# Fetching the mask's rows of the transposed keys through GpSimd's DMA queue instead of SyncE's

## The chip, the cores and the metric

The kernel runs on one core of one Trainium2 chip. The metric is the device time of one execution in microseconds (us). The profile shows one execution by the hardware profiler; its times are counted from the start of the span.

## The reference

The kernel computes one transformer layer in float32, for 16 batches of 100 tokens of width 256, with a context of 361 rows for each batch: cross attention with 16 heads of width 16, and then a soft mixture of 16 experts with 64 slots each.

```python
x = x + xattn(layernorm(x), ctx, ctx, mask, ...)    # 16 heads, 361 keys
x = x + ffn(layernorm(x), ...)                      # 16 experts, soft slots
...
score = einsum('bhqd,bhkd->bhqk', q, k) / sqrt(HD)
score = score + (1.0 - mask) * -1000000000.0
alpha = softmax(score, axis=-1)
```

The mask has one value for each batch and key. It is added to the scores of every head and every query.

## The kernel before

**Stages and order.** The 16 batches are taken in five groups of 2, 2, 4, 4 and 4. For every batch the kernel projects queries and keys and then runs four "units" (`cb` = 0 to 3, four heads each): the scores' maxima (matmuls L681, reduction L686 on VectorE), the corrected queries (L694, L696), the exponentials (L704, L712) and the product with the values (L726). An output projection follows (`out_work`, L627), a second layernorm, and the dispatch to the experts' slots (`dispatch_quarter`: L821, softmax with L881, transposes L889, L899). The experts of a group (L1150 gate and up projections, L1110 down projection) run while the attention of the next group is worked on. All of it is put in order when the program is built: a planner keeps an estimated clock for each engine (`Clock`), holds every piece of work as a generator that tells when it is ready (`Task`), and always takes the next ready one. So each engine has a fixed list of instructions and goes through it in that order; it waits at an instruction until what that one needs is there. Before the first expert the planner fills TensorE's waiting time with matmuls that nobody reads (`warm_up`, L1201), and these too are fixed in number.

**How the mask gets into the scores.** The keys are kept transposed in `kT`, 128 partitions by two halves `oc`, two parities `par` and 361 keys. Each group of 32 partitions holds two heads, of which a parity keeps one and blanks the other, so that blank rows can carry other things: row `MAXROW` carries the maxima, row `MASKROW` the mask. `late_loads` turns the mask into (mask - 1) * 1e9 and stores it in device memory (`mrow_d`, L292). For every batch, `key_work` computes the keys on TensorE (`k_ps`, L546), writes `kT` for `oc` = 0 by VectorE (L557) and for `oc` = 1 by ScalarE (L562), and then issues four small DMAs at L573, one for each (`par`, `oc`), each of which copies the batch's 361 mask values to the four rows that blank heads leave free (5.6 KB). They are issued in the order (0,0), (0,1), (1,0), (1,1), each after the engine that wrote that part of `kT`. The unit `cb` = 2 * `oc` + `par` reads the part that belongs to it.

**Queues.** Before the change SyncE (SP) issues these four DMAs, and nearly all others: the context `c_sb` (L180, L181), the tokens `acc` (L171), the experts' weights `w_all` in pieces of 512 KB (L1084), their biases (L1090) and the results (L1055). GpSimd (POOL) issues only nine small or middling DMAs at the start (mask, biases, layer norm parameters, one scale; L213 to L232) and the slot embeddings `se` (L340, 1 MB, in `parameter_work`), which VectorE's statistics read first (L370, called in `slot_work` at L396). `se` lies in the buffer `ring`, and the profile names it so. GpSimd also computes: reciprocal square roots (L381, helper `rstd`), the scaling of the attention's result (L618), the bias L513, the dispatch weights (L881) and the combine weights (L978, L1004 to L1008).

```python
def parameter_work():
    yield 14.0, 0
    nc.gpsimd.dma_start(
        se, slot_embeds.rearrange("e s d -> (e s) d").rearrange("(c p) d -> p c d", p=P)
    )
```

**Buffers.** `kT` and `c_sb` have two buffers each; for the second group (batches 2 and 3) the keys lie in a part of `ring` instead. Six slots hold experts' weights, and a weight's load is issued as soon as the slot's last reader is done.

Of the kernel before, what the change touches and what calls it, by code (L numbers as in the profile page):

```python
# [118 lines left out]
def xattn_ffn_kernel(  # L119
# [27 lines left out]
    nc = tc.nc  # L147
# [9 lines left out]
    def mm_tile(name):  # L157
        return ps_mm.tile([P, 512], F32, tag="mm", name=name)
# [19 lines left out]
    def load_kv(b):  # L178
        c_sb = two.tile([P, 3, D], F32, tag="c_sb", name="c_sb")
        nc.sync.dma_start(c_sb[:KC, 0:2, :], kv[b, : 2 * KC].rearrange("(c p) d -> p c d", p=KC))  # L180
        nc.sync.dma_start(c_sb[: S2 - 2 * KC, 2, :], kv[b, 2 * KC :])  # L181
        loads[b] = c_sb
        kv_t[b] = max(ck.t["PE"] + 6.0, 5.5)
# [332 lines left out]
    def key_work(b):  # L516

        yield 5.5, 0
        if b + 1 < B and b + 1 not in loads:
            load_kv(b + 1)  # L520
        c_sb = loads[b]
        cT = const.tile([P, KD, S2], F32, tag="cT", name="cT")
        t = [0.0, 0.0]
        for kd in range(KD):
            yield kv_t[b], 1
            ps = mm_tile("c_t")
            for c in range(3):
                n = KC if c < 2 else S2 - 2 * KC
                nc.tensor.transpose(  # L529
                    ps[:, c * KC : c * KC + n],  # L530
                    c_sb[:n, c, kd * P : (kd + 1) * P],
                    ident[:n, :n],
                )
            nc.scalar.copy(cT[:, kd, :], ps[:, :S2])
            t = ck.copy(361, ck.run("PE", 0.33, ck.bank(), kv_t[b]))
            ck.free(t)
        early = group_of[b] == 1
        kT = early_kT[b % 2] if early else None
        for oc in range(KD):
            yield (lambda: max(t, par_t[0], 7.0) if kT is not None or keys_fit(b) else NEVER), 1  # L540
            if kT is None:
                live.add(b)
                kT = two.tile([P, KD, 2, S2], F32, tag="kT", name="kT")
            ps = mm_tile("k_ps")
            for kd in range(KD):
                nc.tensor.matmul(  # L546
                    ps[:, :S2],
                    lhsT=w_sb["wk"][:, kd, oc * P : (oc + 1) * P],
                    rhs=cT[:, kd, :],
                    start=kd == 0,  # L550
                    stop=kd == KD - 1,
                )
            tk = ck.pe(722, t, ck.bank())
            for par in range(2):
                one = slice(par, par + 1)
                if oc == 0:
                    nc.vector.tensor_scalar(  # L557
                        kT[:, oc, par, :], ps[:, :S2], sel[:, one], kb[:, oc, one], ALU.mult, ALU.add
                    )
                    tk = ck.psum_dve(361, tk)  # L560
                else:
                    nc.scalar.activation(  # L562
                        kT[:, oc, par, :],
                        ps[:, :S2],
                        AF.Identity,
                        bias=kb[:, oc, one],
                        scale=sel[:, one],
                    )
                    tk = ck.copy(361, tk)
            ck.free(tk)  # L570
        for par in range(2):
            for oc in range(KD):
                nc.sync.dma_start(  # L573
                    kT.rearrange("(r c) k t s -> r c k t s", c=32)[:, MASKROW[par], oc, par, :],
                    mrow_d[b : b + 1].to_broadcast([4, S2]),
                )
        keys[b] = (kT, tk + 3.0)
        vp = values_of[b] = (early_vpads if early else vpads)[b % 2]
        for c in range(3):

            yield t, 1
            ps = mm_tile("v_ps")
            for kd in range(KD):
                nc.tensor.matmul(  # L584
                    ps[: KC + 1, :D],
                    lhsT=cT[:, kd, c * KC : c * KC + KC + 1],
                    rhs=w_sb["wv"][:, kd, :],
                    start=kd == 0,
                    stop=kd == KD - 1,
                )  # L590
            nc.vector.tensor_tensor(
                vp[: KC + 1, c, :, 0:4:3, :],
                ps[: KC + 1, :D].rearrange("p (x k w) -> p x k w", k=2, w=HD),
                bcs["bv"][: KC + 1, :].rearrange("p (x k w) -> p x k w", k=2, w=HD),
                ALU.add,
            )
            tv = ck.psum_dve(256, ck.pe(512, t, ck.bank()))
            ck.free(tv)
        values_t[b] = tv
# [146 lines left out]
    def keys_fit(b):  # L746
        return len(live) < 2
# [6 lines left out]
    def units(g):  # L754
        last = None

        def finish(u):
            u.values()
            if u.cb == 3 and u.b + 1 in group and u.b + 2 in group:
                fill.append(Task(key_work(u.b + 2), ck))  # L760

        group = range(starts[g], starts[g] + GROUPS[g])
        for b in group:
            for cb in range(4):
                yield (lambda: max(keys[b][1], qps[b][1]) if b in keys and b in qps else NEVER), 0
                yield free_t[0], 0
                u = Unit(b, cb)
                u.maxima()
                if cb == 0 and b % 2 == 1 and b + 1 in group:
                    fill.append(Task(query_work(b + 1), ck))  # L770
                if last:
                    lt = last
                    yield (lambda: values_ready(lt)), 1
                    finish(last)
                yield u.t, 0
                u.queries()
                yield u.t, 0
                u.exponentials()
                last = u
        yield (lambda: values_ready(last)), 1  # L780
        finish(last)
# [422 lines left out]
    group = 0  # L1204
    fill.append(Task(query_work(0), ck))
    fill.append(Task(key_work(0), ck))
    fill.append(Task(bias_work(), ck))
    fill[0].step()
    late_loads()
    while streams["experts"]:  # L1210
# [3 lines left out]
        if group < len(GROUPS) and not streams["units"]:  # L1214
            if group in accs:
                b0 = starts[group]
                if group > 1:
                    fill.append(Task(query_work(b0), ck))
                    fill.append(Task(key_work(b0), ck))
                    fill.append(Task(key_work(b0 + 1), ck))  # L1220
                elif group == 0:
                    fill.append(Task(key_work(1), ck))
                    fill.append(Task(parameter_work(), ck))
                    fill.append(Task(early_work(), ck))
                    fill.append(Task(slot_work(), ck))
                    load_x(1)
                    fill.append(Task(query_work(2), ck))
                    fill.append(Task(key_work(2), ck))
                    fill.append(Task(key_work(3), ck))
                xns[group] = const.tile([N, NG, D], F32, tag="xn", name="xn")  # L1230
                xnTs[group] = const.tile([P, KD, NG * N], F32, tag="xnT", name="xnT")
                streams["units"] = Task(units(group), ck)
                group += 1
# [102 lines left out]
```

## Time and profile before

| | |
|---|---|
| time, median of 3 runs | 1220.04 us (1219.3 to 1221.12) |
| time of the profiled execution | 1216.74 us |
| its span | 1214.9 us |
| TensorE busy | 1191.2 us (98%) |
| VectorE, ScalarE, GpSimd busy | 559.2, 552.1, 148.5 us (46%, 45%, 12%) |
| mean DMA rate | 119 GB/s |
| DMAs `kT<-mrow_d`, and `ring<-mrow_d` for batches 2 and 3 | 56 and 8, by SP |

The profiled execution has 1.84 us outside its span and lies 3.30 us below the median of the runs. TensorE (PE, with PEld for its weight loads) is busy nearly throughout. The other engines have a lot of idle time, which counts only where TensorE, in its fixed order, comes to an instruction whose input is late. In a line of the timeline the first number is the start, the second the duration; in square brackets stand the idle time just before it and what is taken to have ended it. The rows of the DMA issues end with the KB of one and, for GpSimd's queue, the median time from issue to landing.

### The profile page before, as it was taken

Reading aid. Unit: us, or ns where it says so; the run is one execution under the profiler, and the core shown is the slowest. Engines: PE = TensorE matmul, PEld = TensorE weight load, DVE = VectorE, ACT = ScalarE, POOL = GpSimd, SP = SyncE. Lnnn points to the kernel's source line nnn. Section 1 sums busy time; section 2 is a strip of 40 time slices with the busy share of each in tenths; the row PEclk is TensorE's granted clock in tenths of the full one; section 3 lists DMA queues with packets and bytes.
Section 4 is the critical chain, followed back from the end, with each engine's and each line's share of the span. In section 5 each row is a group of like instructions: output and inputs, shape, how many; then the busy total and the mean of one; then the engine's idle time right before and its main releaser. Section 6 shows DMA issues by size and latency. Waiting matters only on the chain.

```text
span 1214.9 us, 24560 instructions
## 1 busy us (share of the span) xinstructions
PE 1191.2 (98%) x10107; PEld 931.7 (77%) x10107; DVE 559.2 (46%) x1328; ACT 552.1 (45%) x1140; POOL 148.5 (12%) x229
## 2 busy tenths in 40 slices
PE   7998999999999999999999999999999999999998
PEld 5877877877787777777777677887778778877876
DVE  5664555557545556744554423447222233322222
ACT  2436454466454466654544446674111347511110
POOL 2110210014000013231000000034000013200000
PEclk9999999999999999999999999999999999999999
DMA  6103556442566441133223142324354332344441
GB/s 161 39 28 94 168 193 196 156 135 73 163 220 192 139 145 44 41 104 113 81 95 110 36 148 71 109 87 130 122 168 141 125 109 83 121 136 147 147 141 53
DMA packets 104184, 144.71 MB, mean 119 GB/s; under 512 B 6284, under 2 KB 62792, under 8 KB 104072
## 3 DMA queue, kind: packets, MB, share of 16 engines
q1 hardware_dynamic: 103216, 141.60, 37.2%
q8 instruction: 80, 1.31, 0.5%
q0 software_dynamic: 576, 1.27, 0.4%
q10 hardware_dynamic: 280, 0.26, 0.1%
q14 instruction: 32, 0.26, 0.1%
HBM read 141.45 MB, written 1.66 MB: 118 GB/s over the span
## 4 chain that ended last, share of the span: by engine, by line
PE 94%; DVE 2%; ACT 2%; DMA 1%; issue 0%; POOL 0%; ACTq 0%; POOLq 0%; DVEq 0%
PE dn L1110 19%; PE gp L1150 19%; PE up L1150 18%; PE sl L899 5%; PE po L1032 4%; PE at L704 4%; PE at L681 4%; PE lg L821 3%; PE k_ps L546 3%; PE cx L726 3%; PE v_ps L584 3%; PE warm L1201 2%; PE o_ps L627 1%; PE d_t L889 1%; DMA kT<-mrow_d 1%; PE c_t L529 1%
## 5 line engine op out<-in xcount | busy, mean ns | idle before, releaser
L1166 DVE SCALAR_TENSOR_TENSOR hT<-up,parT,ge 128x256 f32<-128x256 f32 (+1 forms) x320 | 119.9, 425 | 282.3 <-PE up L1150 194.5
L1150 PE MATMUL gp<-ring,w_all 128*128 128x256 f32 (+1 forms) x1280 | 248.5, 341 | 0.2 <-ACT xnT L657 0.2
L1150 PE MATMUL up<-ring,w_all 128*128 128x256 f32 (+1 forms) x1280 | 246.6, 340 | 0.1
L1161 ACT ACTIVATE ge<-gp,parT 128x256 f32<-128x256 f32 (+1 forms) x320 | 116.7, 429 | 261.5 <-PE gp L1150 260.9
L1110 PE MATMUL dn<-w_all,hT 128*64 128x256 f32 x2048 | 231.8, 381 | 0.0
L1150 PEld LDWEIGHTS gp<-ring,w_all 128*128 128x128 f32 x1280 | 202.7, 191 | 27.5 <-issue 6.4
L1150 PEld LDWEIGHTS up<-ring,w_all 128*128 128x128 f32 x1280 | 203.9, 191 | 21.6 <-issue 1.1
L1110 PEld LDWEIGHTS dn<-w_all,hT 128*64 128x64 f32 x2048 | 142.7, 137 | 76.8 <-issue 7.0
L686 DVE TENSOR_REDUCE mxp<-at 100x4 f32<-100x1444 f32 x64 | 106.3, 1661 | 37.5 <-PE at L681 36.6
L1119 DVE TENSOR_TENSOR ring<-dn,bd_bc 128x512 f32<-128x512 f32 x64 | 44.1, 689 | 153.8 <-PE dn L1110 153.8
L1161 ACT ACT_TABLE_LOAD x61 | 78.3, 1283 | 41.6 <-PE gp L1150 34.8
L712 ACT ACTIVATE aT<-at 121x1200 f32<-121x1200 f32 x64 | 74.9, 1170 | 44.5 <-PE at L704 40.7
L618 POOL TENSOR_TENSOR cxs<-cxs,rs 128x100 f32<-128x100 f32 x63 | 25.1, 399 | 412.1 <-DVE rs L615 336.7
L712 ACT ACT_TABLE_LOAD x39 | 50.0, 1283 | 31.4 <-PE at L704 20.0
L899 PE MATMUL sl<-disp,xn 100*128 100x256 f32 x256 | 61.4, 385 | 1.1 <-ACT disp L892 1.1
L881 POOL TENSOR_TENSOR d_ex<-d_ex,d_sm 128x400 f32<-128x400 f32 x28 | 23.7, 852 | 306.6 <-DVE d_sm L878 259.3
L1032 PE MATMUL po<-ring,lg_all 128*100 128x256 f32 x256 | 59.3, 381 | 0.0
L735 ACT COPY cxs<-cx 128x100 f32<-128x100 f32 x64 | 15.5, 242 | 87.8 <-PE cx L726 87.7
L899 PEld LDWEIGHTS sl<-disp,xn 100*128 100x128 f32 x256 | 47.1, 190 | 9.7 <-ACT disp L892 1.8
L704 PEld LDWEIGHTS at<-q,kT 32*121 32x121 f32 x1344 | 41.2, 182 | 16.9 <-issue 7.9
L704 PE MATMUL at<-q,kT 32*121 32x100 f32 x1344 | 50.6, 280 | 0.7 <-DVE q L696 0.6
L1032 PEld LDWEIGHTS po<-ring,lg_all 128*100 128x100 f32 x256 | 41.7, 167 | 12.0 <-DVE hT L1166 0.5
(148 smaller groups left out, 1323.4 us busy)
## 6 DMA issues: line engine op xcount, KB each, us to landing
w_all<-in_L_ffn_Wg_dram SPq DMA_DIRECT2D x80, 512.0 KB
w_all<-in_L_ffn_Wu_dram SPq DMA_DIRECT2D x80, 512.0 KB
w_all<-in_L_ffn_Wd_dram SPq DMA_DIRECT2D x80, 512.0 KB
bd_bc<-in_L_ffn_bd_dram SPq DMA_DIRECT2D x80, 64.0 KB
c_sb<-in_ctx_dram SPq DMA_DIRECT2D x16, 240.0 KB
c_sb<-in_ctx_dram SPq DMA_DIRECT2D x16, 121.0 KB
acc<-in_x_dram SPq DMA_DIRECT2D x8, 200.0 KB
out_dram<-acc SPq DMA_DIRECT2D x8, 200.0 KB
```

The source lines that it names most:

```text
L546: nc.tensor.matmul(ps[:, :S2], lhsT=w_sb["wk"][:, kd, oc * P : (oc + 1) * P], rhs=cT[:, kd, :], start=kd == 0, stop=kd == KD - 1,)
L681: nc.tensor.matmul(self.at[:N, r, :S2], lhsT=self.q[rows], rhs=self.k[rows], start=True, stop=True)
L686: nc.vector.tensor_reduce(mxv[:, :, m : m + 1], self.at[:N, :, :S2], AX.X, ALU.max, negate=True)
L704: nc.tensor.matmul(self.at[: KC + 1, r, c * N : (c + 1) * N], lhsT=self.k[rows, c * KC : c * KC + KC + 1], rhs=self.q2[rows], start=True, ...
L712: nc.scalar.activation(self.aT[: KC + 1], self.at[: KC + 1, :, : 3 * N], AF.Exp)
L899: nc.tensor.matmul(sl[:, kd * 256 : (kd + 1) * 256], lhsT=xns[g][:, b0 + i, kd * P : (kd + 1) * P], rhs=disp[:, i, :], start=True, stop=True,)
L1032: nc.tensor.matmul(pos[i][:N, :D], lhsT=lg_all[:, slot, 2 * c + i, :], rhs=eouts_of(g, q)[:, c, 2 * p + i, :], start=c == 0, stop=c == 1,)
L1110: nc.tensor.matmul(dn[S * x : S * x + S, i * D : (i + 1) * D], lhsT=hts[x][fc // FB][0].rearrange("p (f b s) -> p f b s", f=FB, s=S)[:, fc ...
L1119: nc.vector.tensor_tensor(eouts_of(g, q)[:, j // 2, 2 * half : 2 * half + 2, :], dn.rearrange("p (b d) -> p b d", d=D), biases[k // 2].uns ...
L1150: nc.tensor.matmul(ps[:, f * T : (f + 1) * T], lhsT=w[:, kd, fc * P : (fc + 1) * P], rhs=slots_of(g, q)[:, j, kd].rearrange("p b s -> p (b ...
L1161: nc.scalar.activation(ge[:, cols], ps[:, cols], AF.Gelu, bias=col(8, e, fc))
L1166: nc.vector.scalar_tensor_tensor(out=hT[:, cols], in0=ps[:, cols], scalar=col(NPAR, e, fc), in1=ge[:, cols], op0=ALU.add, op1=ALU.mult,)
```

## The change

For every batch but the first, the four DMAs at L573 are issued by GpSimd instead of SyncE:

```diff
         for par in range(2):
             for oc in range(KD):
-                nc.sync.dma_start(
+                (nc.gpsimd if b else nc.sync).dma_start(
                     kT.rearrange("(r c) k t s -> r c k t s", c=32)[:, MASKROW[par], oc, par, :],
                     mrow_d[b : b + 1].to_broadcast([4, S2]),
                 )
```

These are 15 times four DMAs. The planner does not count DMAs, so the order of the instructions on TensorE, VectorE and ScalarE stays as it was. SyncE's list loses the 60 DMAs. GpSimd's list gets them at the place where `key_work` reaches them; for batch 1 that is ahead of the load of the slot embeddings (L340), for batches 6 and 10 between two of the multiplications L881, and for batch 12 ahead of an L381.

## The prediction

> **What bounds the kernel now.** I read the page first: TensorE (PE) is busy for 98% of the span and makes up 94% of the chain that ended last. So only time in which PE stands still can be won, and only new stillness of PE can be lost.
>
> ```profile
> PE 1191.2 (98%) x10107; PEld 931.7 (77%) x10107; DVE 559.2 (46%) x1328; ACT 552.1 (45%) x1140; POOL 148.5 (12%) x229
> PE 94%; DVE 2%; ACT 2%; DMA 1%; issue 0%; POOL 0%; ACTq 0%; POOLq 0%; DVEq 0%
> ```
>
> Then PE's timeline, for the maxima L681, the first readers of the mask's rows. Of 64 units four waited, and three of these are the first unit of a batch whose rows had just been ordered:
>
> ```profile
> 19.70 0.87 PE L681 MATMUL at<-kT,qp 32*100 32x361 f32 x8 [0.35 <-DMA kT<-mrow_d]
> 212.50 0.87 PE L681 MATMUL at<-kT,qp 32*100 32x361 f32 x8 [0.18 <-DMA kT<-mrow_d]
> 397.22 0.87 PE L681 MATMUL at<-kT,qp 32*100 32x361 f32 x8 [1.00 <-DVE vpad L591]
> ```
>
> These are batches 0, 4 and 8. The third names VectorE's `vpad`, which L681 doesn't read. What it needs of VectorE, `qp` of L502, was done by 396.10, before PE fell idle at 396.22; a DMA is left. I take all three as waits for the rows: 0.35 + 0.18 + 1.00 = **1.53 us**, all that the mask's rows cost PE (batch 12's first unit, at 578.93, waited for nothing). PE's list of waits has no other DMA but that for `para` at the start: no weight was ever late.
>
> SP's timeline, and the chain at batch 4, show why rows of 5.6 KB take so long: they are queued behind 2 MB of weights and context.
>
> ```profile
> 387.39 0.63 SPq L1084 DMA_DIRECT2D w_all<-in_L_ffn_Wd_dram  x1
> 388.08 0.51 SPq L1090 DMA_DIRECT2D bd_bc<-in_L_ffn_bd_dram  x1
> 388.63 0.60 SPq L180 DMA_DIRECT2D c_sb<-in_ctx_dram  x1
> 389.27 0.37 SPq L181 DMA_DIRECT2D c_sb<-in_ctx_dram  x1
> 390.52 3.41 SPq L573 DMA_DIRECT2D kT<-mrow_d  x4
> ```
> ```profile
> 206.62 5.74 DMA kT<-mrow_d
> ```
>
> The chain gives 5.74 us from the first issue to landing at batch 4; batch 8's must have been about 397.1 - 390.5 = 6.6. By the windows the DMA engines were 0.75 to 1.06 busy in every microsecond from 390 to 395.
>
> **Part 1: the rows on GpSimd's queue.** One issue there costs 0.50 to 0.54 us (the four L228), about SP's 0.48 to 0.60. What counts is the time to landing. The trace has this for GpSimd's small DMAs at the start only:
>
> ```profile
> ring<-in_L_ffn_norm_b_dram POOLq DMA_DIRECT2D x1, 1.0 KB, 5.7
> sc_bc<-in_L_ffn_scale_dram POOLq DMA_DIRECT2D x1, 0.5 KB, 3.4
> ```
>
> 3.4 us is the last of them, issued at 8.06 with nothing of its own queue just ahead; 5.7 and up to 6.3 (mask) are those behind one another, with the DMA engines saturated from 4 to 8 us. So the bounds are 3.4 and 6.3. I take 4.5, nearer to 3.4, since the four rows have nothing ahead of them in their own queue.
> - Batch 4: ordered at 206.6, landed at 211.1 (bounds 210.0 and 212.9), PE there at 212.32: **-0.18** (bounds -0.18, +0.4).
> - Batch 8: ordered at 390.5, landed at 395.0 (393.9 to 396.8), PE there at 396.22: **-1.00** (bounds -1.00, -0.4). The next on PE, `c_t` of batch 9, would come at 397.1 and reads context that went out just ahead of the old rows and so landed by 397.1: nothing to 0.1.
> - Batch 12: 572.9 + 4.5 = 577.4, PE at 578.93: 0 (up to +0.2). Batch 2: GpSimd comes free from an L618 at 81.91, rows at 86.4, PE at 88.39: 0. The others have over 9 us to their first L681.
>
> The row first: two small transfers behind SP's burst took 5.74 and 6.6 us. The Trainium skill, "DMA: Bandwidth & Descriptors", section "Queues, rings and completion order", says that each DMA engine alternates between queues packet by packet; by this the rows pass the weights, and the sum is the one above. Its section "Issuing engines are not separate DMA queues" speaks against the change: all queues share 16 engines and another issuer saves only issue time; by this batches 4 and 8 gain nothing. The trace of before cannot decide it.
>
> **Part 2: GpSimd's own work behind the rows.** GpSimd executes in order; the four issues (4 x 0.52 = 2.1 us) also wait for `kT` from VectorE and ScalarE, and what stands next waits with them. 60 issues add 31 us to an engine busy 148.5 of 1214.9. Next in line, by batch:
> - 6 and 10: an L881. For 6 the rows start at 275.26 and end at 277.34; L881 started at 276.21, so it is 1.13 late and ends at 278.2. Its reader, the transposes L889, comes on PE at 280.21: 2.0 left. Batch 10 has the same distances (459.99, 460.94, 464.94). Cost 0.
> - 11: ScalarE's first `kT` part ends at 499.2, the last issue at 500.8; L881 started at 501.01. Cost 0.
> - 12: ScalarE writes `kT` from 574.61 to 575.80; the issues end at 576.8; L381 started at 574.76, so it is 2.05 late and ends at 577.36. Its reader on VectorE, L648, started at 577.77: 0.4 left. Cost 0 (+0.4 at an issue of 0.7).
> - 2, 3, 4, 5, 7, 8, 9, 13, 14, 15: GpSimd's next work started over 2 us after the rows would be issued. Cost 0.
>
> **Part 3: the slot embeddings.** The load L340 was issued at 9.77. Now the rows of batch 1 stand ahead of it and wait for `kT` (VectorE till 24.17, ScalarE from 24.29 to 25.48): issues at 23.65, 24.95, 25.47, 25.99, and L340 at 26.5. Its reader is VectorE:
>
> ```profile
> 9.77 0.94 POOL L340 DMA_DIRECT2D ring<-n_L_ffn_slot_embeds_dram  x1
> 35.51 0.41 DVE L370 BATCH_NORM_STATS2 st<-ring 128x6 f32<-128x256 f32 x1
> 36.94 1.67 DVE L686 TENSOR_REDUCE mxp<-at 100x4 f32<-100x1444 f32 x1 [0.27 <-PE at L681]
> ```
>
> Two things follow. First, from 10 to 20 us the 1 MB no longer shares the engines with SP's first rows (12.71 to 19.57 for batch 0 in the chain; 2.09 MB moved in these 10 us by the windows, half of it `se`). Batch 0's rows then come before PE does: **-0.35** (bound 0). Second, `se` must land by 35.5. It took 10.0 us, which gives 36.5; L686 has 0.27 of slack, so a landing at X costs X - 35.8: +0.7. But SP, no longer held at L573 until 26.6, issues its three weight loads at 17.8 to 19.3; at the 310 GB/s of the windows from 28 to 34 these, `c_sb` and `acc` (2.3 MB) are through by about 27, and `se` has the engines alone: 1.05 MB / 310 = 3.4, plus the 3.4 of a small DMA, lands at 33.3. I take **0**, bound +0.7.
>
> **Part 4: SP without the rows.** It waited 127 us at L573; now the loads behind go out earlier (at 76 instead of 94.5 before the first experts). PE waited for no weight, so nothing is won; later in the mixed phase loads are held by weight slots anyway.
>
> **Sum:** -0.18 - 1.00 - 0.35 = -1.53 us on the profiled 1216.74 (span 1213.4, time 1215.2). PE's later work is PE-bound, so I keep it all. The same off the median of the runs: 1220.04 - 1.53 = **1218.5 us**, -0.13%. All bounds at their worst: +0.4 - 0.4 + 0.2 + 0.4 + 0.7 = +1.3, so 1221.3.
>
> **One more row.** GpSimd's issues stayed at 0.50 to 0.56 us while VectorE was 1.68 of 2.0 us busy with memsets (2 to 4 us). The Trainium skill, "SBUF — State Buffer", section "SBUF: two separate sides", warns that VectorE's two-port operations shut GpSimd out while it writes descriptors: 620 ns become 3100. By that a batch's issue could grow by 10 us and hold L381 and L881; no row here shows it.
>
> **Rivals.**
> - *The rows land no sooner* (5.5 to 6.3 us, the engines being the same). Batch 4 0 to +0.4, batch 8 -1.0 to -0.4, batch 12 up to +0.2, batch 0 -0.35: about 1219.6. For it: the rows at 5.7 to 6.3; against: 3.4. Chance 25%.
> - *The slot embeddings come late* and VectorE stands at L370: the slower side. If the loads are not through and `se` shares with the 1.9 MB of weights and context, it needs 3.4 + 2.98 MB / 310 = 13.0 (X = 39.5, +3.7) up to 10.0 + 6.2 = 16.2 (X = 42.7, +6.9); with the -1.5 that is 1222.2 to 1225.4. It decides from a landing 10.8 us after the issue (X = 37.3). Against: SP is free from 17.8 on. Chance 15%.
> - *GpSimd is held longer*: issues twice as long (4.2 us a batch) make batch 12's L381 2.1 later (+1.7) and `se` too (28.6 + 6.8 = 35.4, or +2.8 at 10.0): 1220.2 to 1223.0. Chance 10%.
> - *More is won*, by waits that I don't see: below 1217.6, 5%.
> - The forecast as it stands: 45%, though the runs' spread (1219.3 to 1221.12) can carry it past a bound.
>
> **Range and chances.** 0.2% is 2.44 us, about what a measurement of this kernel can tell from no change. Faster by more, below 1217.6: 5% and as much again by spread, 10%. Slower by more, above 1222.5: most of the second rival and some of the third, 18%. Within: 72%. The range, 1217.4 to 1223.5, holds the forecast, the first rival, and the lower parts of the second and third.
>
> **What would show it.** After: no idle time before the L681 near 212 and 396 and at 19; L340 near 26.5, L370 not waiting; L881 of batches 6 and 10 about 1.1 later and L889 not. Wrong if L370 or L648 waits, if the rows' issues on GpSimd exceed 0.6 us, or if the L681 still wait.

## The result and the profile after

The change makes the kernel slower: 1224.88 us (median of 15 runs, 1221.84 to 1228.52) against 1220.04 us for the kernel before (15 runs beside them), ratio 1.0045, 95% interval 1.0032 to 1.0058. That is 4.84 us more, where 1.53 us less was predicted, and it lies outside the predicted range. The profiled execution of after took 1222.76 us with a span of 1221.0 us; that of before had 1214.9 us.

The page of after looks almost like the page of before. TensorE has 1.9 us more of busy time, GpSimd 35.3 us more:

```profile
PE 1193.1 (98%) x10107; PEld 933.0 (76%) x10107; DVE 560.3 (46%) x1328; ACT 553.5 (45%) x1140; POOL 183.8 (15%) x289
PE 93%; DVE 2%; DMA 2%; ACT 2%; issue 0%; POOL 0%; ACTq 0%; POOLq 0%; DVEq 0%
```

PE's timeline shows the loss at two first units and one transpose (start, duration, and in brackets the idle time ahead of it with what ended it):

```profile
214.01 0.87 PE L681 MATMUL at<-kT,qp 32*100 32x361 f32 x8 [2.21 <-DMA kT<-mrow_d]
400.15 1.07 PE L681 MATMUL at<-kT,qp 32*100 32x361 f32 x8 [2.00 <-DMA kT<-mrow_d]
583.90 0.36 PE L653 MATMUL xn_t<-ident,xn 100*128 100x100 f32 x2 [0.84 <-DVE xn L648]
```

The waits that the change was to take away at batches 4 and 8 have grown from 0.18 and 1.00 us to 2.21 and 2.00. TensorE's matmuls are the same 10107 in the same order, so comparing equal instructions in the two traces tells where the 6.1 us of the spans lie: at batch 0's L681 after is 0.56 us ahead of before (19.14 against 19.70), at batch 4's L681 it is 1.51 us behind (214.01 against 212.50), at batch 8's 2.93 (400.15 against 397.22), at an L704 soon after it 4.52 (407.82 against 403.30), at batch 12's L653 5.55 (583.90 against 578.35), and 6.1 at the end.

**The rows land late.** The chain of waits holds the stretch from the first row's issue to its landing, at batch 4 and at batch 8. It is this first row, for `cb` = 0, that PE waits for:

```profile
206.37 7.51 DMA kT<-mrow_d
...
392.72 7.30 DMA kT<-mrow_d
```

On SP's queue batch 4's first row took 5.74 us. Yet GpSimd's queue isn't slow as such: over all 52 rows for `kT` the page gives a median of 2.2 us from issue to landing (last number), and the DMA view of 204 to 216 us alone gives 7.0 as the median of batch 4's four rows.

```profile
kT<-mrow_d POOLq DMA_DIRECT2D x52, 5.6 KB, 2.2
```
```profile
kT<-mrow_d POOLq DMA_DIRECT2D x4, 5.6 KB, 7.0
```

**SP runs ahead.** SP's timeline of after at batch 8 shows what fills the DMA engines in these 7 us. Before, the contexts of batch 10 and the next Wg were issued at 395.65, 396.06 and 396.52, behind the rows:

```profile
390.51 0.63 SPq L180 DMA_DIRECT2D c_sb<-in_ctx_dram  x1
391.18 0.38 SPq L181 DMA_DIRECT2D c_sb<-in_ctx_dram  x1
391.66 0.84 SPq L180 DMA_DIRECT2D c_sb<-in_ctx_dram  x1
392.56 0.37 SPq L181 DMA_DIRECT2D c_sb<-in_ctx_dram  x1
394.91 0.39 SPq L1084 DMA_DIRECT2D w_all<-in_L_ffn_Wg_dram  x1
```

The second pair (361 KB) now goes out ahead of the first row, which GpSimd issues at 392.72, and 512 KB of Wg only 2.2 us after it. The windows show the longer burst at batch 4; the columns are the window, its length, the five engines' busy time, then PE's clock, the DMA engines' share and GB/s. Before:

```profile
210.00:211.00 1.00, 1.00 (x7) 0.94 (x6) 0.37 (x1) 0.00 (x0) 0.00 (x0) 1.00 0.87 176
211.00:212.00 1.00, 1.00 (x7) 0.79 (x5) 0.41 (x2) 0.52 (x1) 0.00 (x0) 1.00 0.51 129
212.00:213.00 1.00, 0.82 (x10) 0.29 (x8) 0.93 (x5) 0.52 (x1) 0.00 (x0) 1.00 0.10 33
```

After:

```profile
210.00:211.00 1.00, 1.00 (x7) 0.84 (x6) 0.49 (x1) 0.36 (x1) 0.00 (x0) 1.00 1.05 246
211.00:212.00 1.00, 0.80 (x4) 0.36 (x2) 0.81 (x2) 0.44 (x2) 0.00 (x0) 1.00 1.08 240
212.00:213.00 1.00, 0.00 (x0) 0.00 (x0) 0.93 (x5) 0.23 (x1) 0.42 (x1) 1.00 1.04 231
213.00:214.00 1.00, 0.00 (x0) 0.02 (x1) 0.08 (x1) 0.00 (x0) 1.00 (x2) 1.00 0.84 207
```

**The clock drops behind the second wait.** In after's windows from 400 us, PE is busy, but at half the clock:

```profile
400.00:401.00 1.00, 0.85 (x8) 0.29 (x8) 0.00 (x0) 0.00 (x0) 0.72 (x1) 0.84 0.62 212
401.00:402.00 1.00, 1.00 (x8) 0.85 (x5) 0.74 (x1) 0.00 (x0) 0.00 (x0) 0.50 0.09 31
402.00:403.00 1.00, 1.00 (x7) 1.00 (x6) 1.00 (x2) 0.81 (x2) 0.00 (x0) 0.50 0.00 0
403.00:404.00 1.00, 1.00 (x7) 1.00 (x6) 0.24 (x1) 0.11 (x1) 0.00 (x0) 0.50 0.00 0
404.00:405.00 1.00, 1.00 (x10) 1.00 (x10) 0.00 (x0) 0.00 (x0) 0.00 (x0) 0.95 0.06 16
```

0.16 + 3 x 0.50 + 0.05 = 1.71 us of full clock are missing. That accounts for the step from 2.93 to 4.52 us (1.59).

**Batch 12.** GpSimd's timeline of after has the rows, then the L381 and L513 that stood behind them. L381's input (L378) was done by 579.15; L381 starts 2.65 us later:

```profile
580.10 1.68 POOL L573 DMA_DIRECT2D kT<-mrow_d  x3 [1.77 <-ACT kT L562]
581.80 0.57 POOL L381 TENSOR_TENSOR rstd<-rstd,neghalf 100x1 f32<-100x1 f32 x1
582.34 1.25 POOL L513 TENSOR_TENSOR acc<-acc,bo_bc 100x512 f32<-100x512 f32 x1
```

So L648 on VectorE, which had run alone before (second line), now runs beside L513 and takes over three times as long (first line, after; in run 2 below it is 1.35 us beside L513 too, in run 8 it is 0.40 behind it):

```profile
582.41 1.35 DVE L648 TENSOR_SCALAR xn<-acc,mv,rstd 100x256 f32<-100x256 f32 x1
```
```profile
577.77 0.40 DVE L648 TENSOR_SCALAR xn<-acc,mv,rstd 100x256 f32<-100x256 f32 x1
```

### The profile page after: what moved, and what is told of

It is laid out like the page before. It is cut to its first block, busy times and chain, and to the rows that moved or that the text cites. A ratio compares the mean times of both kernels' runs of the same rounds, so it can differ in the third digit from the quotient of the medians.

```text
span 1221.0 us, 24571 instructions
## 1 busy us (share of the span) xinstructions
PE 1193.1 (98%) x10107; PEld 933.0 (76%) x10107; DVE 560.3 (46%) x1328; ACT 553.5 (45%) x1140; POOL 183.8 (15%) x289
## 4 chain that ended last, share of the span: by engine, by line
PE 93%; DVE 2%; DMA 2%; ACT 2%; issue 0%; POOL 0%; ACTq 0%; POOLq 0%; DVEq 0%
PE dn L1110 19%; PE gp L1150 19%; PE up L1150 18%; PE sl L899 5%; PE po L1032 4%; PE at L704 4%; PE at L681 4%; PE lg L821 3%; PE k_ps L546 3%; PE cx L726 3%; PE v_ps L584 3%; PE warm L1201 2%; DMA kT<-mrow_d 1%; PE d_t L889 1%; PE o_ps L627 1%; PE c_t L529 1%
## 5 line engine op out<-in xcount | busy, mean ns | idle before, releaser
L881 POOL TENSOR_TENSOR d_ex<-d_ex,d_sm 128x400 f32<-128x400 f32 x28 | 23.8, 855 | 297.8 <-DVE d_sm L878 254.4
L704 PEld LDWEIGHTS at<-q,kT 32*121 32x121 f32 x1344 | 41.1, 182 | 16.9 <-issue 8.2
L681 PE MATMUL at<-kT,qp 32*100 32x361 f32 x448 | 48.7, 504 | 4.6 <-DMA kT<-mrow_d 4.2
L704 PE MATMUL at<-q,kT 32*121 32x100 f32 x1344 | 50.6, 280 | 0.7 <-DVE q L696 0.6
```

Source lines behind the costliest of these rows:

```text
L681: nc.tensor.matmul(self.at[:N, r, :S2], lhsT=self.q[rows], rhs=self.k[rows], start=True, stop=True)
L704: nc.tensor.matmul(self.at[: KC + 1, r, c * N : (c + 1) * N], lhsT=self.k[rows, c * KC : c * KC + KC + 1], rhs=self.q2[rows], start=True, ...
```

## The experiments

Three theories stood at the start. **A**: the rows share the DMA engines with SP's burst, and SP, released from the rows, sends more into that burst, so the rows land later. **B**: GpSimd's queue is late by itself when the DMA engines are full. **C**: the loss is spread over GpSimd's own work behind the rows. Every kernel was timed in five rounds beside the kernel before (in the three sessions its median was 1218.08, 1219.18 and 1218.58 us). All differ from it only in what the diffs show.

**1. One row stays on SP.** The fourth row of each batch holds SP until the last part of `kT` is written.

```diff
-                nc.sync.dma_start(
+                (nc.gpsimd if b and (par, oc) != (1, 1) else nc.sync).dma_start(
```

> Of the four rows of a batch only the last, (par, oc) = (1, 1), stays on SyncE (for every batch); the other three of batches 1 to 15 are on GpSimd. SyncE is again held until the keys are written, so the context of the batch after next and the next weights go out as late as before the change. Theory A (the rows land late because the released SyncE lengthens the burst that they share the DMA engines with): the rows of batches 4 and 8 land when the burst of before ended, so the waits at L681 near 214 and 400 shrink from 2.21 and 2.00 us to 0 to 0.5 and 0.5 to 1.0; no low clock near 400; 1219.5 to 1221.5 us. Theory B (GpSimd's queue is slow under load by itself, whatever SyncE does): both waits stay near 2 us, 1222.5 to 1225 us.

Measured: 1222.66 us, ratio 1.004 (1.0024 to 1.0056). PE waited 2.73 us at batch 4 (chain: 8.03 us from issue to landing) and 1.37 at batch 8. Holding SP in this way didn't help, which at this point spoke for B. But SP's timeline showed that it had not been held long: the contexts of batch 6 went out at 210.77, 2.5 us after the first row (before: 5.3 us after it), and the next Wg at 211.70. The windows show what that meant: in the 8.03 us up to the landing the DMA engines moved 2.08 MB at a share of 1.01, against 1.92 MB in the 7.51 us of after and 1.35 MB at a share of 0.82 in the 5.74 us of before. So what SP issues in the first microseconds behind the row can still delay it. Runs 5 and 9 take this up.

**2 to 4. Which batches, and which queue.** Rows of batches 0, 4, 8 on SP and the others on GpSimd; only 4 and 8 on GpSimd; only 4 and 8 on ScalarE's queue.

```diff
-                nc.sync.dma_start(
+                (nc.gpsimd if b not in (0, 4, 8) else nc.sync).dma_start(
```

> The rows of batches 4 and 8, the first of their groups, are back on SyncE; all others but batch 0 stay on GpSimd. If the loss sits at these two units (theories A and B alike): the waits at L681 are 0.2 and 1.0 us again, the 0.35 of batch 0 stays won, the 0.8 at batch 12 stays lost: 1219.5 to 1221.5 us. Theory C (the loss is spread, by GpSimd's own work that stands behind the rows): 1223 us or more.

```diff
-                nc.sync.dma_start(
+                (nc.gpsimd if b in (4, 8) else nc.sync).dma_start(
```

> The counterpart: only the rows of batches 4 and 8 are on GpSimd, all others on SyncE. Theories A and B: waits of about 2.2 and 2.0 us at L681, a low clock after one or both of them in some executions, 1222 to 1225.5 us; the wait of 0.84 at L653 (batch 12) is gone and the 0.35 of batch 0 is back. Theory C: within 1 us of before.

```diff
-                nc.sync.dma_start(
+                (nc.scalar if b in (4, 8) else nc.sync).dma_start(
```

> Only the rows of batches 4 and 8 are moved, to ScalarE's queue, which is a hardware queue like SyncE's; SyncE is released there as in the change. Theory A: ScalarE's rows share the same lengthened burst, waits of 1 to 2.5 us at L681, 1221.5 to 1225 us. Theory B (a trait of GpSimd's software queue, for instance its completion): the rows land within 5 us, waits under 0.3 us, 1218.5 to 1220 us.

Measured: 1220.80 us, ratio 1.0021 (1.0007 to 1.0034), for all but 0, 4 and 8 on GpSimd; 1222.70 us, 1.004 (1.0025 to 1.0055), for 4 and 8 alone on GpSimd; 1219.46 us, 1.0013 (1.0001 to 1.0024), for 4 and 8 on ScalarE. So two batches of fifteen can carry nearly all of the loss (4.6 of 4.8 us), which is against C (the second run's 2.7 and the third's 4.6 us add up to more than the 4.8 of the change; with their intervals, 0.9 to 4.1 and 3.0 to 6.7 us, they can be parts of it). PE's timeline of the third run has the waits of after:

```profile
215.71 0.87 PE L681 MATMUL at<-kT,qp 32*100 32x361 f32 x8 [2.25 <-DMA kT<-mrow_d]
402.27 0.87 PE L681 MATMUL at<-kT,qp 32*100 32x361 f32 x8 [1.87 <-DMA kT<-mrow_d]
```

With ScalarE as the issuer the waits are 0.34 and 0.30 us. (The time still is 1.4 us above before, 0.1 to 2.9 by the interval; no wait in this trace shows where.) The short waits too fit B, but SP's list explains them otherwise, and shows what the rows do on SP. In the compiled program the DMAs of SP and ScalarE take eight semaphores in turn (the traces' records number them 100 to 107), and each DMA waits until the one eight before it has landed; GpSimd's DMAs have semaphores of their own (108 to 115). Four rows on SP or ScalarE take four of these eight places, so that the next context and the next Wg wait for later transfers to land. Rows on GpSimd take none. In the fourth run the contexts of batch 6 went out at 211.58 and 214.34, in the third at 207.50 and 208.14. So the fourth run keeps the brake, and A and B were still not told apart.

**5. GpSimd's queue with SP's places kept.** SP copies four other rows of `kT` into a spare tile where its own rows stood.

```diff
+    spare = const.tile([4, KD, 2, 340], F32, name="spare")
...
-                nc.sync.dma_start(
+                (nc.gpsimd if b in (4, 8) else nc.sync).dma_start(
...
+                if b in (4, 8):
+                    nc.sync.dma_start(
+                        spare[:, oc, par, :],
+                        kT.rearrange("(r c) k t s -> r c k t s", c=32)[:, 5, oc, par, :340],
+                    )
```

> Rows of batches 4 and 8 on GpSimd's queue as in the third run, and SP copies four rows of kT (340 columns of them, partition 5 of each 32) into a spare tile at the place where its own four rows stood. Nothing of the output changes. So SP again waits for the copies of kT there, and again has four small transfers among the eight that it may have under way (each of its transfers waits until the one eight before it has landed). A (the rows land late because SP, released, sends contexts and weights into the burst sooner): the contexts of batch 6 go out some 5 us after the first row, as before (211.90 after 206.62), the rows land under 6.5 us after their issue, PE's two waits at L681 are under 1.2 us each, and the kernel is within 2 us of before (third run: 4.6 above). B (GpSimd's queue is late by itself when the DMA engines are full): the rows land 7 us or more after their issue, PE waits some 2 us at 214 and at 400, and the kernel stays 3 to 5 us above before.

Measured: 1219.24 us, ratio 1.0001 (0.999 to 1.0013). Four more transfers for each of the two batches, and the loss of the third run no longer shows in the time. SP's timeline, the first row at batch 4 by the chain (the third run's line ahead of this run's) and PE's timeline of this run:

```profile
207.76 3.96 SPq L579 DMA_DIRECT2D spare<-kT  x4
213.38 0.34 SPq L180 DMA_DIRECT2D c_sb<-in_ctx_dram  x1
```
```profile
208.03 7.55 DMA kT<-mrow_d
```
```profile
208.02 6.45 DMA kT<-mrow_d
```
```profile
214.61 0.87 PE L687 MATMUL at<-kT,qp 32*100 32x361 f32 x8 [1.16 <-DMA kT<-mrow_d]
399.70 0.87 PE L687 MATMUL at<-kT,qp 32*100 32x361 f32 x8 [0.57 <-DMA kT<-mrow_d]
```

The rows are on the same queue as in the third run, and the first lands in 6.45 us instead of 7.55 (5.87 instead of 7.17 at batch 8; by the median of the four rows 5.1 instead of 7.2, and 4.7 instead of 6.8), because the contexts come 5.4 us after the first row instead of 0.5 us before it. A holds, and B falls as the cause of the loss. But the first row lands no sooner than on SP, where it took 5.74 us in before and 5.96 in run 8: PE's waits of 1.16 and 0.57 us add up to 1.73, more than the 1.18 of before, so a small part of B may be left.

**6. Contexts out of the burst, rows on SP.** The load of a batch's context moves to the place behind the rows two batches earlier. The planner's due time for the context (`kv_t`) keeps its old place and value, so that the orders on TensorE, VectorE, ScalarE and GpSimd stay the same.

```diff
-        kv_t[b] = max(ck.t["PE"] + 6.0, 5.5)
+        if b < 2:
+            kv_t[b] = max(ck.t["PE"] + 6.0, 5.5)
...
-        if b + 1 < B and b + 1 not in loads:
-            load_kv(b + 1)
+        if b + 1 < B and b:
+            kv_t[b + 1] = max(ck.t["PE"] + 6.0, 5.5)
...
+        if b + 2 < B:
+            load_kv(b + 2)
```

> All rows on SP as before; the context of batch b + 2 is loaded behind batch b's rows instead of batch b + 1's ahead of them, so that the context of batch 5 (361 KB) has landed long before the burst at batch 4. The orders on TensorE, VectorE, ScalarE and GpSimd stay the same. A (what is in the burst ahead of the rows sets when they land): 361 KB less at the 300 GB/s of the burst is 1.2 us, so the rows of 4 and 8 land some 1.2 us sooner; PE's waits there (0.18 and 1.00 before) fall to what VectorE ends next, 0 to 0.7 as in the second run: 0 to 1 us faster than before, no more. B (the queue's own manner): says nothing of rows on SP, no change.

Measured: 1217.28 us, ratio 0.9987 (0.9976 to 0.9998), 1.9 us below before's median: more than expected, but the interval reaches into it. PE's timeline shows no idle time ahead of the two L681 (L684 in this file):

```profile
216.04 0.87 PE L684 MATMUL at<-kT,qp 32*100 32x361 f32 x8
...
400.36 0.87 PE L684 MATMUL at<-kT,qp 32*100 32x361 f32 x8
```

So the waits that the change was after, the 1.18 us at batches 4 and 8, go away when 361 KB are taken out from ahead of the rows, without another queue. Whether the time falls by as much isn't shown (see the end).

**7. The same contexts, rows of 4 and 8 on GpSimd.** The sixth run's diff and the third's together.

> The same move of the contexts, with the rows of batches 4 and 8 on GpSimd's queue (third run with 361 KB less ahead of the rows, but SP as free as there). A: the rows land about 1 us sooner than in the third run (7.0 us there), PE's waits at batches 4 and 8 fall from 2.25 and 1.87 to about 1 each, and the kernel is 1 to 3 us above before. B: landing 7 us and waits of about 2 us as in the third run, 3 to 5 us above before.

Measured: 1221.45 us, ratio 1.0023 (1.0012 to 1.0034), 2.3 us above before, as A said. The waits were a miss for A as I had sized it, though: 1.82 and 2.36 us, with the first rows landing in 7.12 and 7.66 us (medians of the four 6.2 and 6.4). SP was free here, and sent batch 6's context at 206.71 and 207.50 and, in the place of the other context, the next Wg (512 KB) at 208.25, all ahead of the first row at 208.82. Taking one transfer out of the burst doesn't help when nothing keeps the next from taking its place.

**8. The twelve batches that have time.** Rows of 0, 4, 8, 12 on SP, the others on GpSimd.

```diff
-                nc.sync.dma_start(
+                (nc.gpsimd if b % 4 else nc.sync).dma_start(
```

> Rows of batches 0, 4, 8 and 12 on SP, the other twelve on GpSimd's queue: the second run with batch 12 also back on SP. If the second run's excess over before (2.6 us, of it 0.83 at batch 12 by the trace) lies at batch 12, where L513 then runs beside L648 of VectorE, this run is within 1.5 us of before and its trace has no wait of PE at L653. C (the change costs a little at every batch, by GpSimd's own work behind the rows): 1.5 to 3 us above before, with no place that stands out.

Measured: 1219.12 us, ratio 1.0001 (0.9988 to 1.0014), and no wait at L653. Twelve batches on GpSimd's queue cost and give nothing that shows (1.5 us less to 1.7 more by the interval), so C falls as the main cause; the second run's loss lies most likely at batch 12, of which its trace shows 0.83 us of waiting at L653.

**9. Places alone.** As run 5, but SP's four small transfers read the mask in device memory, and so wait for no copy of `kT`.

```diff
-                        kT.rearrange("(r c) k t s -> r c k t s", c=32)[:, 5, oc, par, :340],
+                        mrow_d[b : b + 1, :340].to_broadcast([4, 340]),
```

> As the fifth run (rows of batches 4 and 8 on GpSimd's queue), but SP's four small transfers into the spare tile read the mask rows in DRAM (340 columns) and so wait for no copy of kT; what stays of them is that each takes one of the eight transfers that may be under way, so that the contexts of batch 6 and the next Wg wait for later ones to land. A1 (the places among the eight are the brake): contexts of batch 6 some 4 to 5 us behind the row's issue as in the fifth run, next Wg near 214, rows land in about 5 us, PE's waits 1.2 us or less, within 1.5 us of before. A2 (SP's wait for the copies of kT is the brake): contexts of batch 6 near 208 as in the third run, rows after 7 us, waits of some 2 us, 3 to 5 us above before.

Measured: 1219.41 us, ratio 1.0007 (0.999 to 1.0025). The contexts of batch 6 still went out 4.8 us behind the first row (GpSimd's at 212.88):

```profile
212.55 3.16 SPq L579 DMA_DIRECT2D spare<-mrow_d  x4
217.69 0.34 SPq L180 DMA_DIRECT2D c_sb<-in_ctx_dram  x1
```

The first rows landed in 6.80 and 6.00 us (medians of the four 5.4 and 4.5); PE waited 1.50 us at batch 4, somewhat over the 1.2 expected, and at batch 8 0.70 us for VectorE. So the brake is the places among the eight, not SP's wait for `kT`. It also fits run 1, where the one row on SP took one place instead of four.

**10. Runs 6 and 8 together.**

> The move of the contexts of the sixth run with the eighth run's split: rows of batches 0, 4, 8 and 12 on SP, the other twelve on GpSimd's queue. If the twelve are worth nothing either way, this gives the sixth run's time again (ratio 0.9976 to 0.9998 there) and PE waits nowhere at 214 or 400; if the gain of the sixth run was chance, the ratio lies about 1.000.

Measured: 1218.46 us, ratio 0.9984 (0.9965 to 1.0004), and no wait at batches 4 and 8. The estimate repeats the sixth run's, but this interval still holds 1.

## Why the prediction was wrong

**What bounds the kernel, and the three waits (right).** PE's order stayed the bound, and the waits named were those that moved.

**Part 1, the landing of the rows (wrong; this step failed).** "So the bounds are 3.4 and 6.3. I take 4.5, nearer to 3.4, since the four rows have nothing ahead of them in their own queue." The rows took 7.51 and 7.30 us, beyond the upper bound. The two rows of the trace came from the start of the kernel, and the estimate took the burst as before had it. Two things were missing. With SP's places kept (run 5) the first rows still took 6.45 and 5.87 us: a full burst costs 1.4 to 2.0 us more than the 4.5. With SP released (run 3) they took 7.55 and 7.17, another 1.1 to 1.3. Batch 4 was put at -0.18 and came to +2.03 (2.21 - 0.18); batch 8 at -1.00 and came to +1.00 (2.00 - 1.00).

The prediction weighed two rules of the Trainium skill, "DMA: Bandwidth & Descriptors". By the one ("Queues, rings and completion order": the engines alternate between queues packet by packet), as it was read, small rows on a queue of their own pass the weights; here, in a full burst, four of them took 7.0 us (median) instead of 2.2. By the other ("Issuing engines are not separate DMA queues") another issuer gains nothing; run 5 agrees, with 1.73 us of waits in the new queue against 1.18 in the old one. What decided the sign is a third thing: the transfers left behind on the old queue came sooner.

**Part 4, SP without the rows (wrong; what made it a loss).** "PE waited for no weight, so nothing is won." That is true, and it asks only what SP's release wins. It doesn't ask what the earlier loads collide with. The rows were SP's brake, by four of its eight places; without it 361 KB more went out ahead of the rows and 512 KB of Wg just behind them. Runs 3, 5 and 9 show it: same queue, brake back, loss no longer seen.

**The clock (not in the sum at all).** A wait of PE was priced at its length. One of the two waits in after's trace, and the one of 1.87 us in the third run, cost 1.71 us more.

**Batch 12 in part 2 (wrong, small).** "0.4 left. Cost 0": L381 was 2.65 us behind its input, near the 2.05 predicted for its delay; but L513 behind it moved too, into L648, which went from 0.40 to 1.35 us. Every instruction behind a moved one moves, not only the next. PE waited 0.84 us. Run 8 has the wait gone with batch 12's rows back on SP. The section "SBUF: two separate sides" of "SBUF — State Buffer", cited for the issues, warns of GpSimd and VectorE shutting one another out; the overlap of L513 and L648 is where such a thing shows here, while the issues stayed at 0.56 to 0.68 us.

**The rest of part 2, and part 3 (right).** For batch 6 the rows end at 279.35 and L881 starts at 279.38, late as predicted, and the L889 that reads it waits for nothing. L340 started at 26.38 (predicted 26.5) and L370 at 34.95 without waiting:

```profile
26.38 0.95 POOL L340 DMA_DIRECT2D ring<-n_L_ffn_slot_embeds_dram  x1
```

**Batch 0's 0.35 us (came, but not shown as an effect).** The wait is gone in after. It is gone in the third, fifth, sixth, seventh and ninth too, where batch 1's rows are on SP and stand ahead of nothing on GpSimd, and in the fourth it is 1.10 us. It varies from one execution to the next.

**The rivals.** "The rows land no sooner" was nearest, but it ended at 6.3 us; none had the rows landing later. The second rival's 1222.2 to 1225.4 holds the measured time, but by luck: L370 waited for nothing. Of the 6.1 us between the two spans some 1.1 were not traced: 0.4 between batches 4 and 8, 0.2 between 8 and 12 and 0.5 behind 12.

## What to carry to other kernels

A small transfer in a queue of large ones can be a brake on them: before moving it, list what goes out sooner without it, and ask what that collides with, the moved transfer first of all. To get a small transfer through a burst, take out what stands ahead of it and can go earlier (in runs 6 and 10 no wait was left), and keep something that holds the next transfer back. Price a new wait of TensorE above its length where its clock may fall, and follow everything that stands behind an instruction put into another engine's list, not only the next one.

## What the runs showed of the hardware

**A short wait can halve the clock, at a fixed price.** In the one-microsecond windows of all twelve profiled executions TensorE's clock is full or half, or a mean of the two where a window holds the change. Each drop inside the kernel has the same size: some 3.4 us at half clock, 1.70 to 1.71 us lost, or two such stretches in a row (3.41 to 3.42) or three (5.12). The clock changes on a fixed beat: all its changes inside one trace lie whole multiples of 3.413 us apart (in after it is half from 55.94 to 59.36 and from 400.69 to 404.10, and the two starts are 344.75 us, 101 such stretches, apart). The wait of 2.35 us that every one of these kernels has ahead of an L889 near 102 us was followed by a drop in 6 of 12, the wait of 2.02 us ahead of another L889 near 115 us in 2 of 12, the wait of 1.37 us ahead of an L704 near 155 us in 5 of 12, and the waits of 1.8 to 2.8 us at batches 4 and 8 in 2 of 7. The longest of these, 2.73 us, had none, and the one of 1.87 us had one. How a wait lies on the beat counts for much. With each trace cut into stretches of 3.413 us along its own changes, the stretches at full clock in which PE was idle for over 0.65 of the time were followed by half clock in 5 of 5 cases, those with 0.40 to 0.59 in 10 of 24, those with 0.20 to 0.40 in 0 of 39. The wait of 2.00 us lay in one stretch (idle 0.59), the one of 2.73 us was shared by two (0.32 and 0.48). The second run's windows at the wait near 102 us show a drop, with PE idle and then slow:

```profile
102.00:103.00 1.00, 0.00 (x0) 0.00 (x0) 0.97 (x3) 0.00 (x0) 0.00 (x0) 1.00 0.00 0
...
105.00:106.00 1.00, 1.00 (x7) 1.00 (x6) 0.00 (x0) 0.58 (x1) 0.00 (x0) 0.50 0.00 0
106.00:107.00 1.00, 1.00 (x7) 0.98 (x7) 0.00 (x0) 0.00 (x0) 0.00 (x0) 0.50 0.00 0
```

The Trainium skill, "TensorE: Matmul & The Clock Gate", section "Part 1: The HAM clock gate", has a free-running window of 3413 ns and a clock that is full or half; both agree with the 3.4 us and the 0.50 seen here. It gives one idle window of about 3.4 us as what lowers the clock; here waits of 1.37 to 2.35 us did so in some executions. Between 0.40 and 0.59 the idle share alone doesn't decide, and what else does is open.

**A busy TensorE can lose its clock too.** All twelve traces have one, two or three half-clock stretches that begin between 52.6 and 56.5 us, with no wait of over 0.4 us ahead of them. There, or just ahead, PE runs L429, 32 matmuls of a single column each. The profile calls it busy, and before's clock is half from 56.49 to 59.90:

```profile
52.56 3.73 PE L429 MATMUL cb_ps<-parT,seT 128*128 128x1 f32 x32
```

That these thin matmuls are the cause was not tried.

Most of the spread of the runs comes from these drops. Taking span x (1 - granted clock) off each run's time cuts the standard deviation of before's 32 runs beside runs 5 to 8 from 1.8 to 0.6 us, and leaves means of 1213.2 us for before, 1216.4 for run 3, 1214.1 for run 5, 1212.9 for run 6, 1216.0 for run 7 and 1213.6 for run 8; for run 10 1212.8 against 1213.7 for before beside it. So run 6 is 0.3 us and run 10 0.9 us below before by this count, nearer to the expected 0 to 1 us than run 6's median says, and the rest of its lead of 1.9 us may be the luck of the clock. Run 5 is 0.9 us above before by it, where run 3 was 3.2 above: most of the loss is gone, not all.

**Packets of GpSimd's queue.** The four rows of a batch made 128 packets on GpSimd's queue (about 180 bytes each) and 32 on ScalarE's, for the same 22 KB. Whether the finer cut adds to the landing time in a burst stays open. With SP's places kept, the first row at batch 4 took 6.45 us on GpSimd's queue (run 5) against 5.74 on SP (before) and 4.94 on ScalarE's (run 4), but ScalarE issued it later in the burst.

**A full share with less moved.** In the stretched burst the DMA engines show a share of 1.04 to 1.08 at 231 to 246 GB/s (after, 210 to 213 us), where before had 0.99 at 304 to 324 GB/s (208 to 210 us). Two queues at once aren't needed for it: before, with the rows on SP, has a share of 0.87 at 176 GB/s from 210 to 211 us. Why the same share moved less was not tried.
